# A two-layer graph and expert network on one core: zeros and edge windows written beside the expert sets, gathers and products in another order

## The chip, the core and the metric

The kernel runs on one core of a Trainium2 chip. Its engines are TensorE (PE, matrix products, with its weight loads shown as PEld), VectorE (DVE), ScalarE (ACT), GpSimd (POOL) and SyncE (SP, which here only issues DMAs). The metric is the device time of one execution in microseconds (us). The kernel before takes 968.34 us, the median of five runs between 967.43 and 974.61.

## The reference

There are 3125 nodes of 256 features (float32) and 50000 directed edges, which come sorted by their target `dst`. Cut to what matters, the reference computes

```python
# 1. first graph layer: of each node's incoming edges only the last counts
agg = zeros_like(x).at[dst].set(layernorm(x)[src])
x = x + concatenate((layernorm(x), agg), 1) @ L0_gnn_W.T + L0_gnn_b
# 2. first expert layer: 8 experts of 1024 hidden units, the two best of each node
g = layernorm(x) @ Wg.T + bg;  top 2, softmax over the two
x = x + sum_e combine[:, e] * (relu(layernorm(x) @ W1[e].T + b1[e]) @ W2[e].T + b2[e])
# 3. second graph layer, over all edges
t1  = x @ hW1;  msg = (t1[src] + x[src] * x[dst] @ hW2) / (sqrt(out_deg[src]) * sqrt(out_deg[dst]))
e   = where(in_cnt > 0, t1 + segment_sum(msg, dst), 0) + hb
x   = x + normalized(leaky_relu(e))
# 4. second expert layer: router over 8 experts of 256 hidden units, exact gelu, the two best
x   = x + sum_e combine2[:, e] * (gelu(layernorm(x) @ w1[e] + b1[e]) @ w2[e] + b2[e])
```

## The kernel before

The nodes lie in 25 tiles of 128 rows. Half 0 is tiles 0 to 10, half 1 is tiles 11 to 24. The instructions of each engine run in the order in which the program emits them; this order is written out by hand. All the DMAs named here are issued by SP's queue or, where they gather or scatter by index, by POOL's, and each of these two queues issues in order too.

**The front, 0 to about 60 us.** The edges are read in 13 groups. For each, DVE makes one-hots, PE counts them, and `edge_rows` writes a piece of `etab` (L437), a table in DRAM from which the last edge of a node can be gathered. In the same loop `turn_next` turns the normalized rows of x, multiplies them with the half of the weights that belongs to the neighbour, and writes the products `Z` to the table `ztab` in DRAM (L359). Six DMAs at the start of this block load `wrows` (L389 to 391), the edges laid out as 1560 overlapping windows of 128; L488 writes them to `wtab` in DRAM. `clear_steps` (L247, L250) writes zeros to a table in DRAM, eight groups of 128 rows to a DMA; in this loop it clears the two tables `ytab` (2.9 MB for half 0, 3.5 MB for half 1) into which the first expert layer scatters its results. One step of it follows each group of edges.

**The gathers of half 0, 53 to 123 us.** `picked(t0, t1)` gathers for each tile the rows `er` of `etab` that hold the last edges (`last_edges`, L539, POOL), picks the edge out of them on DVE (`pick_edge`, L545) and makes the neighbours' numbers `nbr` (`neighbours`, to L553). `near(t)` gathers the neighbours' rows of `ztab` (`near_z`, L557, POOL), adds them on DVE (`plus_near`, L575) and takes the statistics of the normalization, for some tiles on ACT. `plus_own(t)` adds the node's own product: four matmuls of PE and one addition on DVE (L566, L569). `other()` is the same product for the next tile of half 1, whose result stays in `hT` and `own_pre` and is read out by ACT (L571, L572). `root` and `finish` normalize up to four tiles on ACT and store them to `xtab` in DRAM (`store_rows`, L590, SP; the three stores are those of tiles 0 to 3, 4 to 7 and 8 to 10). Behind `gate_of_norm` and `sc.best` the routing of half 0 (`route_steps`, its last step on DVE is L870) gives every expert its rows.

**The first expert layer, 123 to 586 us.** 16 sets: the eight experts for half 0 with up to 3 tiles of rows, then the eight for half 1 with up to 4. Before the first set `take` gathers rows of `xtab` (L1021, POOL), which needs all three stores and the routing. In a set a first phase multiplies the turned rows with the first weights (L1067), ACT applies relu into `hid` (L1071), `turn` turns the next set's rows (L1040), and a second phase multiplies `hid` with the second weights (L1081), tile by tile; behind each tile DVE adds the bias (`tensor_add` into `y`, L1086), and POOL scatters `y` to `ytab` (L1090). The weights come by SP (`load_weights`, L951 to 959).

Between these matmuls the program calls `slot()`. Each call advances the generator `beside_first` by one `yield`, that is, it emits the next piece of other work. A set of half 0 has 29 slots (17 in and behind the first phase, 12 in the second), a set of half 1 has 33; there are 496 in all. In this order `beside_first` holds: the rest of half 0's routing; `first_layer_rest`, the first graph layer of half 1; its scores and routing; `windows`, which gathers the windows `win` of `wtab` (L1208) and works on them with DVE (L1217 and the lines behind it, 12 yields after the gathers); `total_in` (its wait for the load `degin` is at L1267, a matmul on PE at L1273); `count_edges`, which builds the matrix of edge counts `atab`; the combination of half 0's results and its statistics (reads `ytab` at L1131, an addition at L1144, the square root at L1542 on ACT); and the addition of the first results of half 1. That last part holds 14 additions on DVE, one for a tile. What is left of the generator after the last slot is emitted then.

**After that.** From 587.86 us PE multiplies the edge counts, loaded by SP (`at`, L1646) and converted by ACT (`wide`, L1796), with the rows (L1800). The fourth of these loads (`at[3]`) reuses memory that the last of the 14 additions reads, and so waits for it. Behind it in SP's queue stand loads of half 1's second results (`second`, L1131). From about 830 us the second expert layer follows.

The clears in the kernel before, one step behind each group of edges:

```python
            if g > 1 and clears and next(clears[0], 0) == 0:
                clears.pop(0)
```

Of the kernel before, what the change touches and what calls it, by code (L numbers as in the profile page):

```python
# [8 lines left out]
F32 = mybir.dt.float32  # L9
# [70 lines left out]
def groups(n, size, first=0):  # L80
    return [(a, min(a + size, n)) for a in range(first, n, size)]
# [28 lines left out]
def gnn_ffn_kernel(ctx: ExitStack, tc: tile.TileContext, x, src_a, src_d, dst_d, dst_row,  # L110
# [121 lines left out]

    wtab = dram.tile([NB, 2, P], I32, name="wtab")

    deg = keep.tile([P, T], F32)
    rooted = keep.tile([P, T], F32)
    none = keep.tile([P, T], I32)
# [141 lines left out]
        nc.vector.tensor_add(X[:, t, :], X[:, t, :], gbt)  # L379

    with tc.tile_pool(name="edges", bufs=2, reuse_waits="tile") as ep:
        WR = NB // 120
        assert WR * 120 == NB
        wrows = ep.tile([120, WR, 2, P], I32, bufs=1)
        for i, a in enumerate((src_a, dst_row)):
            def edges(first, dims):
                return bass.AP(tensor=a.tensor, offset=a.offset + first, ap=dims + [[1, P]])

            nc.sync.dma_start(out=wrows[:119, :, i, :], in_=edges(0, [[WR * B, 119], [B, WR]]))  # L389
            nc.sync.dma_start(out=wrows[119:, :WR - 1, i, :], in_=edges(119 * WR * B, [[1, 1], [B, WR - 1]]))  # L390
            nc.sync.dma_start(out=wrows[119:, WR - 1, i, :], in_=edges(E - P, [[1, 1]]))
        clears = [c for h in range(2) for c in (clear_steps(tabs1[h][1]),)]
        less_mean = ep.tile([P, 2, P], F32, bufs=1)
        iota_2 = ep.tile([P, P], BF16, bufs=1)
        nc.vector.tensor_copy(iota_2, iota_i[:, :P])
# [71 lines left out]
        for g in range(NG):  # L467
            one_hots(g + 2)
            while len(rooted_z) > 1:
                scale_z(*rooted_z.pop(0))  # L470
            if g == NG - 2:
                nc.vector.tensor_scalar(gbase, iota_i[:, :NG], 256.0, None, OP.mult)
            if g == NG - 1:
                last_key(0, 0, NG - 2)
            hot, tiles = hots.pop(g)
            n = min(GE, CD - g * GE)
            pg = bank([P, 2, T], F32, "sb" if g % 2 else "sa", 1)
            for j in range(n):
                nc.tensor.matmul(pg, hot[:, j, :], tiles[:, j, :, :T], start=(j == 0), stop=(j == n - 1))
            nc.scalar.copy(sums[:, g], pg)  # L480
            if 2 <= g < 2 + len(parts_e):
                edge_rows(*parts_e[g - 2])
            if g == 1:
                gates_of_bias()
            while turned[0] < int((g + 1) * STEP):
                turn_next()
            if g == NG - 2:
                nc.sync.dma_start(out=wtab.rearrange("(p r) i l -> p r i l", p=120), in_=wrows)  # L488
            if g > 1 and clears and next(clears[0], 0) == 0:
                clears.pop(0)  # L490
        last_key(1, NG - 2, NG)
        nc.vector.tensor_tensor(last[:, 0], last[:, 0], last[:, 1], OP.max)
        last = last[:, 0]
# [19 lines left out]
        while rooted_z:  # L513
            scale_z(*rooted_z.pop(0))
        nc.vector.tensor_tensor(pre, Z[:, :, DZ + 2:], gates[:, 1:2, :].to_broadcast([P, T, NE]), OP.add)
        assert not any(next(c, 1) is None for c in clears)
    of_turn.close()

    def norm_stats(get, tiles_, tag, mv=None):
# [24 lines left out]
    def pick_edge(pick, i, er, t):  # L544
        nc.vector.scalar_tensor_tensor(pick[:, i, :], er[:, 0, :], node[:, t:t + 1], er[:, 1, :],  # L545
                                       OP.is_equal, OP.mult)
# [779 lines left out]
    with tc.tile_pool(name="ffn", bufs=2, reuse_waits="tile") as fp:  # L1326
# [7 lines left out]
        gp_route = ExitStack()  # L1334
        rp = gp_route.enter_context(tc.tile_pool(name="route", bufs=1, reuse_waits="tile"))
        with tc.tile_pool(name="gnn", bufs=2, reuse_waits="tile") as gp:
            def picked(t0, t1):
                pick = gp.tile([P, 4, P], F32, name="pick", bufs=1)
                for t in range(t0, t1):
                    er[t] = last_edges(eb, t, 8)  # L1340
                    pick_edge(pick, t - t0, er[t], t)
                neighbours(gp, pick, t0, t1)

            loaded1 = {k: [] for k in range(2)}
            sum2 = gp.tile([P, n], F32, bufs=1)

            def near(*tiles_):
                for t in tiles_:
                    plus_near(t, near_z(gp, t, 8))
                    if t in STATS_BY_ACT:  # L1350
                        stat_by_act(gp, mv2, sum2, t)
                    else:
                        stat(X[:, t, :], mv2, t)

            def other():
                t = others.pop(0)
                plus_own(t, own_pre[:, t - n, :])

            def finish(t0, t1):

                scales(mv2, t0, t1)
                xn = gp.tile([P, 4, D], F32, name="xn5")
                for t in range(t0, t1):
                    normed_by_act(xn[:, t - t0, :], X[:, t, :], mv2, t)
                store_rows(tabs1[0][0], 0, t0, t1, xn)

            sc = Scores(rp, 0, 1, pre[:, :n])
            picked(0, 4)
            for t in range(3):
                plus_own(t)  # L1370
            picked(4, 8)
            for t in range(3, 7):
                plus_own(t)
            picked(8, n)
            for t in range(7, n):
                plus_own(t)
            for _ in range(3):
                other()
            near(0, 1, 2, 3)
            root(mv2, 0, 4)  # L1380
            other()
            other()
            near(4, 5)
            finish(0, 4)
            other()
            near(6, 7)
            root(mv2, 4, 8)
            other()
            other()
            near(8, 9)  # L1390
            finish(4, 8)
            near(10)
            root(mv2, 8, n)
            for t in range(n, n + 8):
                er[t] = last_edges(eb, t, 8)
            finish(8, n)
            gate_of_norm(gp, 0, n)
            run(sc.best(0, n))
            for k in range(2):
                for part in range(2):  # L1400
                    load_weights(fp, weights1, HC, slice(k, k + 1), loaded1[k], part)
            routed1[0] = Routed()
            route_rest = route_steps(routed1[0], rp, 0, None, 1, sc)
            for i, _ in enumerate(route_rest):
                if routed1[0].done or i in OWN_AT:
                    while others:
                        other()
                        if not routed1[0].done:
                            break
                if routed1[0].done:  # L1410
                    break
            assert not others
# [51 lines left out]
        def beside_first():  # L1464
            yield from route_rest
            gp_route.close()
            yield from first_layer_rest()
            of_edges.close()
            with tc.tile_pool(name="route", bufs=1, reuse_waits="tile") as rp:
# [3 lines left out]
            with tc.tile_pool(name="codes", bufs=1, reuse_waits="tile") as qp:  # L1473
                qs = qp.tile([P, GW * P, 2], BF16)
                cs = qp.tile([P, GW * P, 2], BF16)
                yield from windows(qs, cs)
                with tc.tile_pool(name="onehots", bufs=2, reuse_waits="tile") as hp:
                    yield from total_in(hp, into)
# [670 lines left out]
```

## Time and profile before

| | value |
|---|---|
| median of five runs | 968.34 us (967.43 to 974.61) |
| the profiled execution: its own time | 971.0 us |
| its span (what the profile shows) | 969.3 us |
| TensorE clock granted, mean over the span | 0.954 of full speed |
| PE busy | 864.3 us, 89% of the span |
| DVE, ACT, POOL busy | 584.4, 401.4, 313.2 us |
| moved by DMA | 162.02 MB, 167 GB/s over the span |
| first matmul of the first expert set | 123.42 us |
| starts of sets 4, 5, 6 | 211.50, 240.58, 272.51 us |
| last bias addition of the first expert layer | 586.23 us |

The profile records one execution. A span is counted from its start, so a time like "at 240.58 us" is a place in this execution. The page cuts the span into 40 slices of 24.2 us and gives for each the busy share in tenths. A wait is shown as the instruction that waited, its line, the engine or DMA and tile that released it, and the sum, number and longest of such waits. A stretch is shown as busy microseconds of each engine with the number of its instructions in brackets, then the granted clock of PE, the busy share of the DMA engines (a little over 1 where records overlap) and GB/s.

### The profile page before, as it was taken

What the parts mean: (1) busy time and instruction counts of PE and PEld (TensorE: products, weight loads), DVE (VectorE), ACT (ScalarE), POOL (GpSimd) and SP (SyncE); (2) the same over time, 40 slices, a digit from 0 to 9 for tenths busy, and PEclk for the clock granted to TensorE, in tenths of its full rate; (3) what the DMA queues carried; (4) which work ended last, traced back from release to release, by engine and by line L of the source; (5) the groups of instructions that cost most, each with busy time, mean ns of one, the idle gap of its engine ahead of it and who ended that gap; (6) DMA issues with size and microseconds to landing.
All of it is one profiled execution on the core that took longest, in us unless ns stands there. A gap on an engine that the chain in (4) does not pass through costs nothing. (4 is left out here: it accounts for less than half of the span.)

```text
span 969.3 us, 13802 instructions
## 1 busy us (share of the span) xinstructions
PE 864.3 (89%) x4803; PEld 641.4 (66%) x4803; DVE 584.4 (60%) x1516; ACT 401.4 (41%) x935; POOL 313.2 (32%) x325
## 2 busy tenths in 40 slices
PE   8937499999699999999999998999999998899980
PEld 7825267666477676676666666789987785657660
DVE  8967566884456555555535526665559665584563
ACT  4833322321136556656632335745564652222110
POOL 2045356622323231341131110011004744274450
PEclk9989699999989999999999999999999999799995
DMA  7993935752456867566354335221013327467964
GB/s 217 275 297 103 294 124 181 236 183 78 137 126 211 304 213 239 197 199 210 125 189 143 107 104 169 69 68 40 20 45 106 120 88 235 118 202 207 312 237 160
DMA packets 124111, 162.02 MB, mean 167 GB/s; under 512 B 21106, under 2 KB 101900, under 8 KB 123911
## 3 DMA queue, kind: packets, MB, share of 16 engines
q1 hardware_dynamic: 104319, 115.05, 37.8%
q0 software_dynamic: 13968, 34.16, 10.8%
q10 hardware_dynamic: 5744, 11.82, 3.2%
q8 instruction: 40, 0.66, 0.3%
q14 instruction: 40, 0.33, 0.1%
HBM read 98.07 MB, written 64.18 MB: 167 GB/s over the span
## 5 line engine op out<-in xcount | busy, mean ns | idle before, releaser
L1081 PE MATMUL y<-w,hid 128*128 128x256 f32 (+4 forms) x1120 | 280.7, 394 | 11.4 <-DVE y L1086 11.1
L1067 PE MATMUL big<-xs,w 128*128 128x380 f32 (+3 forms) x640 | 261.1, 536 | 5.5 <-ACT hid L1071 3.5
L1081 PEld LDWEIGHTS y<-w,hid 128*128 128x128 f32 (+4 forms) x1120 | 199.2, 188 | 44.4 <-DVE y L1086 15.2
L1090 POOL DMA_INDIRECT ytab<-y,put x112 | 125.1, 1117 | 233.2 <-DVE y L1086 212.9
L1071 ACT ACTIVATE hid<-big,bt 128x380 f32<-128x380 f32 (+3 forms) x160 | 97.7, 613 | 222.5 <-PE big L1067 199.2
L1067 PEld LDWEIGHTS big<-xs,w 128*128 128x128 f32 x640 | 114.5, 193 | 68.6 <-issue 28.5
L1796 ACT CAST wide<-at 128x384 fp32r<-128x384 uint8 (+1 forms) x225 | 94.9, 484 | 46.4 <-PE sb L1800 19.1
L1086 DVE TENSOR_TENSOR y<-y,b2t 128x256 f32<-128x256 f32 (+2 forms) x112 | 47.4, 424 | 99.2 <-PE y L1081 98.4
L1021 POOL DMA_INDIRECT g<-xtab,take x56 | 57.9, 1033 | 138.5 <-PE tr L1040 111.2
L1308 PEld LDWEIGHTS <-hq 128*128 128x128 bf16 x800 | 57.1, 98 | 59.6 <-issue 42.6
L1288 DVE TENSOR_TENSOR hq<-qs,iota_b 128x2048 bf16<-128x2048 bf16 x50 | 61.2, 1223 | 55.4 <-PE sb L1308 55.4
L1800 PE MATMUL sa<-wide,parts 128*128 128x512 f32 (+2 forms) x200 | 72.0, 364 | 1.7 <-ACT wide L1796 1.7
L1800 PE MATMUL sb<-wide,parts 128*128 128x512 f32 (+2 forms) x200 | 72.0, 364 | 0.0
L1800 PE MATMUL big<-wide,parts 128*128 128x512 f32 (+1 forms) x300 | 69.5, 381 | 1.7 <-ACT wide L1796 1.7
L1309 ACT CAST at<-sa 128x400 uint8<-128x400 f32 x100 | 49.0, 490 | 40.7 <-PE sa L1308 40.7
L1309 ACT CAST at<-sb 128x400 uint8<-128x400 f32 x100 | 49.0, 490 | 34.6 <-PE sb L1308 33.8
L1041 DVE COPY xs<-tr 128x380 f32<-128x380 f32 (+3 forms) x64 | 35.5, 595 | 45.2 <-PE tr L1040 45.2
L1800 PEld LDWEIGHTS big<-wide,parts 128*128 128x128 f32 x300 | 54.1, 188 | 9.3 <-ACT wide L1796 2.1
L1612 POOL TENSOR_TENSOR XX<-XX,kept 128x256 f32<-128x256 f32 x14 | 10.5, 774 | 122.3 <-DVE kept L533 122.3
L1291 DVE TENSOR_TENSOR hc<-cs,iota_b 128x1600 bf16<-128x1600 bf16 x50 | 49.3, 985 | 0.0
L566 PE MATMUL big<-gWo,hT 128*128 128x264 f32 x100 | 29.1, 450 | 18.8 <-DVE XX L569 14.9
L539 POOL DMA_INDIRECT er<-etab,chunk x25 | 24.6, 984 | 55.3 <-DMA ztab<-Z 37.0
(363 smaller groups left out, 1175.8 us busy)
## 6 DMA issues: line engine op xcount, KB each, us to landing
w<-in_fW SPq DMA_DIRECT2D x32, 1024.0 KB
ytab<-zero_b SPq DMA_DIRECT2D x10, 1024.0 KB
atab<-at ACTq DMA_DIRECT2D x25, 400.0 KB
at<-atab SPq DMA_DIRECT2D x25, 400.0 KB
w<-in_mw SPq DMA_DIRECT2D x32, 256.0 KB
xtab<-zero_b SPq DMA_DIRECT2D x7, 1024.0 KB
y<-ytab SPq DMA_DIRECT2D x12, 512.0 KB
rows<-xtab SPq DMA_DIRECT2D x8, 512.0 KB
```

The source lines that it names most:

```text
L1021: nc.gpsimd.indirect_dma_start(out=g, out_offset=None, in_=tabs[h][0], in_offset=bass.IndirectOffsetOnAxis(ap=routed[h].column(c)[0], axis=0))
L1067: nc.tensor.matmul(ph[:, :many], w1[:, i, c * P:(c + 1) * P], turned[k][:, i, :many], start=(i == 0), stop=(i == KD - 1))
L1071: nc.scalar.activation(hid[:, c, :many], ph[:, :many], act, bias=bt[:, 0, c:c + 1])
L1081: nc.tensor.matmul(py[:m], hid[:, c, j * P:j * P + m], w2[:, c, :], start=(c == 0), stop=(c == nh - 1))
L1086: nc.vector.tensor_add(y[:m], py[:m], b2t[:m])
L1090: dma = nc.gpsimd.indirect_dma_start(out=tabs[h][1], out_offset=into, in_=y[:m], in_offset=None, bounds_check=2 * tokens(layer, h) - 1, oo ...
L1288: nc.vector.tensor_tensor(in_pairs(hq), pairs(qs[:, mine], P), in_pairs(iota_b[:, None, :].to_broadcast([P, n, P])), OP.is_equal)
L1291: nc.vector.tensor_tensor(in_pairs(hc), pairs(cs[:, mine], C), in_pairs(iota_b[:, None, :C].to_broadcast([P, n, C])), OP.is_equal)
L1308: nc.tensor.matmul(pa[:, j], hq[:, g + j, :], hc[:, g + j, :], start=True, stop=True)
L1309: nc.scalar.copy(at[:, :, W * (g0 + g):W * (g0 + g + 4)].rearrange("p i (g w) -> p i g w", w=W), pa.rearrange("p g i w -> p i g w"))
L1796: nc.scalar.copy(wide[:, :j1 - j0, t - t0, :], at[t][:, j0:j1])
L1800: nc.tensor.matmul(sums[g][d][:, :n], parts[:, i, k, d * P:(d + 1) * P], wide[:, i - j0].rearrange("p t l -> p (t l)")[:, :n], start=(i == ...
```

## The change

The work that is computed stays the same; its place in the queues changes.

- The edge windows no longer pass through `wrows`: `window_rows` copies them from DRAM to `wtab` in DRAM with ten DMAs, at the start of the work beside the expert sets, behind the rest of half 0's routing. It yields eight times.
- The zeros of half 0's `ytab` are written behind `finish(4, 8)`, so that in SP's queue they stand between the store of tiles 4 to 7 and that of tiles 8 to 10. The zeros of half 1's `ytab` are written beside the sets, before `windows`, in four yields.
- Gathers of `er` for tiles 0 to 7 come first, then the gathers from `ztab` for tiles 0 to 3, then `er` for 8 to 10, and `ztab` for 4 to 7 and 8 to 10. `pick` has two buffers.
- Own products of half 1 (`other`): 3, 2, 1 and 2 at four places and the rest among the routing before; 2, 3, 2 and 2 now and the rest among the routing. `near(0, 1)` comes before `picked(8, n)`.
- The weights of the first expert are loaded behind `finish(0, 4)`, and only the second expert's behind `sc.best`.

Line numbers of the kernel behind the change are six lower for most of the code (L1217 becomes L1211), and sixteen higher near the end (L1646 becomes L1662).

```diff
@@ -232,6 +232,16 @@
 
     wtab = dram.tile([NB, 2, P], I32, name="wtab")
 
+    def window_rows():
+
+        for i, a in enumerate((src_a, dst_row)):
+            for b0, b1 in groups(NB - 1, 400):
+                nc.sync.dma_start(out=wtab[b0:b1, i, :],
+                                  in_=bass.AP(tensor=a.tensor, offset=a.offset + b0 * B, ap=[[B, b1 - b0], [1, P]]))
+                yield
+            nc.sync.dma_start(out=wtab[NB - 1:, i, :],
+                              in_=bass.AP(tensor=a.tensor, offset=a.offset + E - P, ap=[[P, 1], [1, P]]))
+
     deg = keep.tile([P, T], F32)
     rooted = keep.tile([P, T], F32)
     none = keep.tile([P, T], I32)
@@ -379,17 +389,6 @@
         nc.vector.tensor_add(X[:, t, :], X[:, t, :], gbt)
 
     with tc.tile_pool(name="edges", bufs=2, reuse_waits="tile") as ep:
-        WR = NB // 120
-        assert WR * 120 == NB
-        wrows = ep.tile([120, WR, 2, P], I32, bufs=1)
-        for i, a in enumerate((src_a, dst_row)):
-            def edges(first, dims):
-                return bass.AP(tensor=a.tensor, offset=a.offset + first, ap=dims + [[1, P]])
-
-            nc.sync.dma_start(out=wrows[:119, :, i, :], in_=edges(0, [[WR * B, 119], [B, WR]]))
-            nc.sync.dma_start(out=wrows[119:, :WR - 1, i, :], in_=edges(119 * WR * B, [[1, 1], [B, WR - 1]]))
-            nc.sync.dma_start(out=wrows[119:, WR - 1, i, :], in_=edges(E - P, [[1, 1]]))
-        clears = [c for h in range(2) for c in (clear_steps(tabs1[h][1]),)]
         less_mean = ep.tile([P, 2, P], F32, bufs=1)
         iota_2 = ep.tile([P, P], BF16, bufs=1)
         nc.vector.tensor_copy(iota_2, iota_i[:, :P])
@@ -484,10 +483,6 @@
                 gates_of_bias()
             while turned[0] < int((g + 1) * STEP):
                 turn_next()
-            if g == NG - 2:
-                nc.sync.dma_start(out=wtab.rearrange("(p r) i l -> p r i l", p=120), in_=wrows)
-            if g > 1 and clears and next(clears[0], 0) == 0:
-                clears.pop(0)
         last_key(1, NG - 2, NG)
         nc.vector.tensor_tensor(last[:, 0], last[:, 0], last[:, 1], OP.max)
         last = last[:, 0]
@@ -513,7 +508,6 @@
         while rooted_z:
             scale_z(*rooted_z.pop(0))
         nc.vector.tensor_tensor(pre, Z[:, :, DZ + 2:], gates[:, 1:2, :].to_broadcast([P, T, NE]), OP.add)
-        assert not any(next(c, 1) is None for c in clears)
     of_turn.close()
 
     def norm_stats(get, tiles_, tag, mv=None):
@@ -1334,19 +1328,28 @@
         gp_route = ExitStack()
         rp = gp_route.enter_context(tc.tile_pool(name="route", bufs=1, reuse_waits="tile"))
         with tc.tile_pool(name="gnn", bufs=2, reuse_waits="tile") as gp:
-            def picked(t0, t1):
-                pick = gp.tile([P, 4, P], F32, name="pick", bufs=1)
+            def gather_rows(t0, t1):
                 for t in range(t0, t1):
                     er[t] = last_edges(eb, t, 8)
+
+            def picked(t0, t1):
+                pick = gp.tile([P, 4, P], F32, name="pick", bufs=2)
+                for t in range(t0, t1):
                     pick_edge(pick, t - t0, er[t], t)
                 neighbours(gp, pick, t0, t1)
 
+            z = {}
+
+            def gather_near(t0, t1):
+                for t in range(t0, t1):
+                    z[t] = near_z(gp, t, 8)
+
             loaded1 = {k: [] for k in range(2)}
             sum2 = gp.tile([P, n], F32, bufs=1)
 
             def near(*tiles_):
                 for t in tiles_:
-                    plus_near(t, near_z(gp, t, 8))
+                    plus_near(t, z[t])
                     if t in STATS_BY_ACT:
                         stat_by_act(gp, mv2, sum2, t)
                     else:
@@ -1365,30 +1368,41 @@
                 store_rows(tabs1[0][0], 0, t0, t1, xn)
 
             sc = Scores(rp, 0, 1, pre[:, :n])
+            gather_rows(0, 8)
             picked(0, 4)
-            for t in range(3):
+            gather_near(0, 4)
+            for t in range(4):
                 plus_own(t)
+            for _ in range(2):
+                other()
             picked(4, 8)
-            for t in range(3, 7):
+            gather_rows(8, n)
+            gather_near(4, 8)
+            for t in range(4, 8):
                 plus_own(t)
+            near(0, 1)
             picked(8, n)
-            for t in range(7, n):
+            gather_near(8, n)
+            for t in range(8, n):
                 plus_own(t)
             for _ in range(3):
                 other()
-            near(0, 1, 2, 3)
+            near(2, 3)
             root(mv2, 0, 4)
-            other()
-            other()
+            for _ in range(2):
+                other()
             near(4, 5)
             finish(0, 4)
-            other()
+            for part in range(2):
+                load_weights(fp, weights1, HC, slice(0, 1), loaded1[0], part)
             near(6, 7)
             root(mv2, 4, 8)
-            other()
-            other()
+            for _ in range(2):
+                other()
             near(8, 9)
             finish(4, 8)
+            for _ in clear_steps(tabs1[0][1]):
+                pass
             near(10)
             root(mv2, 8, n)
             for t in range(n, n + 8):
@@ -1396,9 +1410,8 @@
             finish(8, n)
             gate_of_norm(gp, 0, n)
             run(sc.best(0, n))
-            for k in range(2):
-                for part in range(2):
-                    load_weights(fp, weights1, HC, slice(k, k + 1), loaded1[k], part)
+            for part in range(2):
+                load_weights(fp, weights1, HC, slice(1, 2), loaded1[1], part)
             routed1[0] = Routed()
             route_rest = route_steps(routed1[0], rp, 0, None, 1, sc)
             for i, _ in enumerate(route_rest):
@@ -1464,6 +1477,7 @@
         def beside_first():
             yield from route_rest
             gp_route.close()
+            yield from window_rows()
             yield from first_layer_rest()
             of_edges.close()
             with tc.tile_pool(name="route", bufs=1, reuse_waits="tile") as rp:
@@ -1473,6 +1487,8 @@
             with tc.tile_pool(name="codes", bufs=1, reuse_waits="tile") as qp:
                 qs = qp.tile([P, GW * P, 2], BF16)
                 cs = qp.tile([P, GW * P, 2], BF16)
+                for _ in clear_steps(tabs1[1][1]):
+                    yield
                 yield from windows(qs, cs)
                 with tc.tile_pool(name="onehots", bufs=2, reuse_waits="tile") as hp:
                     yield from total_in(hp, into)
```

## The prediction

> **What bounds the kernel now.** I read the page's slices first, for where TensorE (PE) is not busy, then the chain that ended last (it covers only the closing stores, so it decides nothing here), then the time by stretches of a few us, then the waits in the stretches where PE falls short.
>
> ```profile
> PE   8937499999699999999999998999999998899980
> PEclk9989699999989999999999999999999999799995
> DMA  7993935752456867566354335221013327467964
> ```
>
> A slice is 24.2 us. PE is at 9 nearly everywhere from 123 us to the end: there the kernel is bound by PE, and an edit pays only through stretches in which PE stands still or runs at a lower clock. The weak slices are 48 to 121 us (digits 3 7 4: the gathers, with the DMA engines busy), one 6 with a lower clock at 242 to 267 us, and an 8 at 582 us. The first stretch is seen best here:
>
> ```profile
> core 0: us, PE busy (x) PEld busy (x) DVE busy (x) ACT busy (x) POOL busy (x), PEclk, DMA share, GB/s
> 48.00:52.00 4.00, 4.00 (x39) 3.30 (x38) 3.72 (x14) 3.14 (x12) 0.00 (x0) 1.00 1.05 348
> 64.00:68.00 4.00, 0.00 (x0) 0.00 (x0) 0.35 (x1) 0.00 (x0) 1.19 (x2) 0.50 0.97 246
> 76.00:80.00 4.00, 3.48 (x12) 2.48 (x12) 3.01 (x10) 0.00 (x0) 0.93 (x1) 0.82 0.03 10
> 100.00:104.00 4.00, 0.00 (x0) 0.00 (x0) 2.53 (x11) 2.60 (x6) 2.61 (x3) 0.50 0.69 220
> 116.00:120.00 4.00, 0.00 (x0) 0.00 (x0) 0.76 (x3) 0.00 (x0) 3.09 (x4) 0.80 1.07 358
> ```
>
> At 48 to 72 us the DMA engines are the bound (share 0.96 to 1.05): the zeros of both ytab halves, issued at 31.9 to 52 us, are ahead of the last etab, ztab and wtab stores. At 76 to 80 us they stand empty. From 96 to 120 us they are full again, with the weights. The sets of the first expert layer, one row each:
>
> ```profile
> 146.06:167.30 21.24, 21.24 (x88) 15.76 (x86) 13.77 (x36) 4.62 (x8) 15.23 (x16) 1.00 0.61 200
> 211.50:240.58 29.08, 26.53 (x207) 18.43 (x206) 16.53 (x49) 5.99 (x10) 7.19 (x7) 1.00 0.34 105
> 240.58:272.51 31.93, 24.53 (x92) 17.84 (x89) 16.28 (x23) 4.62 (x8) 13.00 (x14) 0.84 0.42 123
> ```
>
> A half-0 set takes 21.24 us when nothing holds it. Set 5 takes 31.93. Its waits:
>
> ```profile
> DVE w L1217 <- DMA win<-wtab,begin_i: 15.3, 1, 15.3
> POOL ytab L1090 <- DVE y L1086: 15.5, 3, 13.4
> PE y L1081 <- DVE y L1086: 7.4, 1, 7.4
> ```
>
> VectorE (DVE) waits in order at L1217 for the seven gathers `win` (243.0 to 251.5 us, landed 256.59). The bias additions L1086 queue behind that wait and behind the window steps of about 1.09 us that follow it; the first runs at 265.54. PE runs out of buffers, stands 7.40 us, and restarts at half clock (16 matmuls in 6.67 us, against 3.62).
>
> **The change, part by part.** Side work advances by one yield per slot among the expert matmuls. window_rows adds 8 yields and the clears of half 1 add 4, so everything behind them comes 12 slots later (8 slots between the two). It adds 10 DMA issues and removes 7. Four places decide.
>
> *Front, 53 to 123 us.* Without the zeros the er rows need not land at 62.7, 67.0, 70.8, and ztab lands about 71 (69.5 to 73) instead of 78.7: the 6.4 MB of zeros alone are 18.5 us of DMA at 345 GB/s, but the rest of this stretch's work (one-hots on DVE to 53 us, first pick at 61.62 at the earliest) hides most of it. Gathers near 0 to 3 start 7 us earlier. But gathers er 8 to 10 now follow them on GpSimd, at 1.25 us an issue, and the picks of tiles 8 to 10 wait for them: they end near 83, as before (83.3). Behind that the chain on ScalarE (ACT) loses one own product of half two (0.5 us) from between; the gate comes 0.5 us sooner (at most 3). New is what stands in SP's queue ahead of the store of xtab rows of tiles 8 to 10: store 0 to 3 (0.52 MB), expert 0's weights (2.23), store 4 to 7 (0.52), the zeros (2.88), its own 0.39, and some 0.4 of er rows: 6.95 MB from about 97.5 us. At the 345 GB/s of the full stretches (337 to 358) that is 20.1 us, plus 2 to 2.5 to land: 120. The first expert gathers L1021 wait for all three stores; they began at 115.48, when the routing (L870) was done, so they begin at about 120. Behind them the first turn comes 6.2 us later as before (115.48 to 121.67): 125.7 instead of 121.67. Loss 4. Ends: 385 GB/s, as in a later stretch full of zeros (xtab<-zero_b, 364 to 410), gives a loss of 2.3; 246, the slowest full row above, gives 28.3 us and a loss of 12.6; a gain of 1 if the store passes the zeros. I take 345 because its rows are of the same mix, weights and zeros, at the same share.
>
> [...]
>
> *Sets 4 and 5.* The win gathers move from slot 1 of set 5 to slot 13, the wait (L1217) from slot 13 to slot 25, behind the bias additions of the second tile. PE then has its buffers while DVE waits. Set 5 loses 31.93 - 21.24 = 10.7; I give back 1.6 to the next wait in line (L1267 `degin`, 8.6 us long in set 6, whose PE users L1273 come with it) and 0.5 to a late addition: gain 8.6 (5 to 10.5). Set 4 loses 29.08 - 26.53 (its PE busy time), of which the exp table load and a wait at L1199 leave its first phase: gain 1.3 (0 to 2). Together 9.9.
>
> *Set 13.* Its first phase takes 16.9 us (501.14 to 518.0) against 12.46 in its neighbours:
>
> ```profile
> DVE XX L1144 <- DMA y<-ytab: 4.3, 1, 4.3
> ACT stats L1542 <- DVE stats L1541: 2.7, 1, 2.7
> PEld big L1067 <- ACT hid L1071: 3.7, 2, 3.2
> ```
>
> The square root L1542 on ACT waits for statistics whose rows come by DMA, loads a table (1.28 us), and the relus L1071 stand behind it; PE waits for hid, then runs at 0.87 and 0.70 of its clock. Twelve slots later L1542 stands behind the last relu of that phase. Gain 4.3 of 4.4 (2 to 4.6).
>
> *End of the experts.* The 14 combines of first results (0.42 us each on DVE) stood all before the last bias addition (586.23). Now four do, and nine are issued after the last slot. The load at[3] (L1646) waits for the last of them: 584.3 before, about 586.9 + 10 x 0.42 = 591.1 now; it landed 2.9 later, so the dense product that began at 587.86 begins at about 594.8, 6.9 later. It had about 3.3 us of stalls of its own in its first 40 us (35.9 of work in 39.2), which the later start absorbs, and `second` loads (L1131), which sit behind at[3] in SP's queue, feed a DVE chain that goes with them: net loss 4 (2.3 to 7).
>
> The clears of half 1 and the DMA copies of wtab in the sets cost nothing: the DMA share there is 0.34 to 0.71. If that cover failed, the weights of a set (1.1 MB a piece, 3.2 us at 345 GB/s) would be late. Losing wrows' six loads (8.86 to 25.9) moves nothing: DVE is busy 19.8 of 20 us there.
>
> Sum: -4 + 9.9 + 4.3 - 4 = +6.2 saved. The profiled run took 971.0 (span 969.3 and 1.7 around it), so 964.8 by its own time. It stands 2.7 above the median of 968.3; none of that lies in a stall that the change moves, so against the median: 962.
>
> **The rivals.**
> *Slower: the zeros in front of the last xtab store.* The other three terms gain 10.2. A later first turn uses that up when the store lands at 125.7 (268 GB/s) and it is slower by over 0.5% from 130.5 on (226 GB/s). For it: 231 and 220 GB/s were what moved at 96 to 104 us. At 220 it is 31.6 us, landing at 131.4, loss 15.9: 974. Against: the share was 0.69 to 0.76 there, so the engines lacked work; full rows with zeros in them gave 337 to 348.
> *No change: the stall keeps its length.* DVE still waits at L1217 for gathers that take 13.6 us to land, and the next bias additions queue behind it, now between tiles two and three or in set 6's second phase. For: the wait is not shortened, only shifted. Against: 25 to 29 slots leave the last addition only. If half of 8.6 and half of 4.3 stay lost: 968.5.
> *Larger gain: the store is not late.* If the er rows and zeros move at 385 and the gate comes 3 us sooner, the front is even and the end loses 2.3: 956.
> The change does what it says; there is no rival in that.
>
> **How the numbers follow.** A measurement can tell about 0.5% (4.8 us) from no change: 963.5 and 973.2 are the bounds. Forecast (958 to 966, middle 962) 0.47; stall kept 0.25; zeros too slow 0.15; larger gain 0.13. Faster: all of the last and 0.37 of the first: 0.50. Slower: the zeros' 0.15 and 0.04 from the stall with a front at its low end: 0.19. Same: 0.31. The range 954 to 975 leaves out the tails of the outer cases, 0.1 each.
>
> **What would show it.** Right: `near` starts at 70 to 73; the third xtab store lands after the routing is done and L1021 starts at 119 to 121; set 5 takes under 24 us with L1217's wait intact but no PE wait at L1081 over 2 us; set 13's first phase under 13 us; L1646's fourth load issued at 590 to 592, first product at 594 to 596. Wrong: L1021 at 115 (no delay) or over 125 (rival one); PE waiting for DVE y in set 5 or 6 again (rival two); at[3] issued at 585, which would mean the combines were not behind the last addition.

## The result, and the profile after

The changed kernel takes 972.97 us (median of 52 runs) where the kernel before takes 970.94 (94 runs): ratio 1.0025, 95% interval 1.0015 to 1.0035. It is slower by about 2.4 us: clear of the noise, but within the half per cent that the prediction counts as no change. Forecast was 962, faster by 0.65%. The profiled execution after took 975.57 us, span 973.8.

The slices of the changed kernel, 24.3 us each:

```profile
PE   7975389998999999999999996999999998899980
PEclk9997679999899999999999998999999999799995
DMA  6143946566546776666445225121013327367964
```

The 6 at 242 us is gone, and a 9 stands there, but an 8 stands one slice earlier (219 us), and a new 6 at 584 us, where before had an 8; the granted clock has an 8 there now, where it had a 9. In the front PE's 3 7 4 has become 7 5 3: the work has moved forward, and the hole ends later. The DMA row has fallen at 24 to 73 us from 9 9 to 1 4, where the zeros and the window rows were written.

What the slices hold in microseconds, from the start of the first matmul of each set to the next (the last column is an experiment, told below):

| stage | before | after | before with twelve empty yields |
|---|---|---|---|
| first expert matmul at | 123.42 | 128.47 | 123.39 |
| sets 0 to 3 | 88.08 | 90.04 | 89.79 |
| set 4 | 29.09 | 30.99 | 30.95 |
| set 5 | 31.93 | 23.83 | 23.83 |
| sets 6 to 12 | 228.63 | 227.86 | 227.95 |
| set 13 | 31.51 | 29.88 | 30.38 |
| sets 14 and 15, to the end of the last bias addition | 54.00 | 53.99 | 54.00 |
| from there to the first dense product | 1.21 | 7.56 | 7.53 |
| first dense product at | 587.86 | 592.62 | 587.82 |

**The front.** The same stretches as shown of before, with the one behind them:

```profile
100.00:104.00 4.00, 0.00 (x0) 0.00 (x0) 3.41 (x15) 1.58 (x3) 0.00 (x0) 0.50 0.95 344
116.00:120.00 4.00, 0.00 (x0) 0.00 (x0) 0.00 (x0) 0.00 (x0) 0.94 (x1) 0.50 1.00 353
120.00:124.00 4.00, 0.00 (x0) 0.00 (x0) 0.00 (x0) 0.00 (x0) 2.97 (x4) 0.50 1.08 338
```

The DMA engines are full from 96 us on, at 344 GB/s and not at 220, and from 116 to 124 us no engine works but POOL, which issues gathers. The wait ahead of them, from the list of waits:

```profile
POOL g L1015 <- DMA xtab<-xn: 21.0, 1, 21.0
```

The store of tiles 8 to 10 was issued at 109.71 us, behind the zeros, and landed when POOL went on, at 118.87; the routing had been done since 113.3.

**Sets 4 and 5.** The same rows as before:

```profile
218.51:249.50 30.99, 25.98 (x146) 18.46 (x144) 17.09 (x58) 6.20 (x10) 7.36 (x8) 0.89 0.65 216
249.50:273.33 23.83, 23.83 (x156) 17.29 (x153) 7.89 (x18) 4.62 (x8) 11.13 (x12) 1.00 0.47 150
```

Set 5 now has PE busy in all of its 23.83 us. Set 4 has PE idle for 5.0 us and its clock at 0.89. POOL's timeline in set 4 and the waits there show whom it waits for:

```profile
235.94 1.03 POOL L1084 DMA_INDIRECT ytab<-y,put  x1 [3.16 <-DVE y L1080]
237.28 0.97 POOL L1015 DMA_INDIRECT g<-xtab,take  x1 [0.31 <-issue]
239.40 1.01 POOL L1084 DMA_INDIRECT ytab<-y,put  x1 [1.14 <-DVE ff L1176]
240.71 0.97 POOL L1015 DMA_INDIRECT g<-xtab,take  x1 [0.30 <-issue]
241.70 0.90 POOL L1178 IOTA w<- 128x896 int32 x1
```

```profile
PE sa L1193 <- DVE less L1187: 4.2, 1, 4.2
DVE first L1180 <- POOL w L1178: 3.4, 1, 3.4
```

`windows` begins with an iota on POOL (L1184 before). There it ran at 218.05 us, in the first phase of the set, with no scatter or gather ahead of it. Twelve slots later it stands behind two scatters and two gathers of the second phase, and POOL, in order, reaches it at 241.70. DVE waits for it, then makes `less`; PE, in order, waits for `less` with expert matmuls behind it, and runs its next matmuls at half clock (four in 2.05 us against 1.11).

**The end.** The waits at 577 to 600 us and the additions on DVE:

```profile
ACT wide L1812 <- DVE XX L1138: 10.0, 1, 10.0
PE sa L1816 <- ACT wide L1812: 8.0, 1, 8.0
```

```profile
584.64 0.42 DVE L1080 TENSOR_TENSOR y<-y,b2t 80x256 f32<-80x256 f32 x1 [1.45 <-PE y L1075]
584.98 4.03 DVE L1138 SCALAR_TENSOR_TENSOR XX<-first,weight,XX 128x256 f32<-128x256 f32 x10
```

Ten additions of first results run behind the last bias addition, then the load they held, and PE stands for 8.0 us.

### The profile page after: what moved, and what is told of

Same layout as the page of the kernel before. It is cut to its first block, busy times and chain, and to the rows that moved or that the text cites. A ratio compares the mean times of both kernels' runs of the same rounds, so it can differ in the third digit from the quotient of the medians.

```text
span 973.8 us, 13826 instructions
## 1 busy us (share of the span) xinstructions
PE 866.6 (89%) x4803; PEld 644.0 (66%) x4803; DVE 584.8 (60%) x1516; ACT 401.7 (41%) x935; POOL 315.8 (32%) x325
## 5 line engine op out<-in xcount | busy, mean ns | idle before, releaser
L1075 PE MATMUL y<-w,hid 128*128 128x256 f32 (+4 forms) x1120 | 275.9, 390 | 5.1 <-DVE y L1080 4.6
L1061 PEld LDWEIGHTS big<-xs,w 128*128 128x128 f32 x640 | 112.9, 192 | 61.3 <-issue 24.3
L1816 PE MATMUL sa<-wide,parts 128*128 128x512 f32 (+2 forms) x200 | 74.2, 374 | 8.0 <-ACT wide L1812 8.0
L1816 PE MATMUL sb<-wide,parts 128*128 128x512 f32 (+2 forms) x200 | 74.2, 374 | 0.0
L1816 PEld LDWEIGHTS sa<-wide,parts 128*128 128x128 f32 x200 | 39.2, 196 | 12.4 <-issue 8.4
```

Source lines behind the costliest of these rows:

```text
L1061: nc.tensor.matmul(ph[:, :many], w1[:, i, c * P:(c + 1) * P], turned[k][:, i, :many], start=(i == 0), stop=(i == KD - 1))
L1075: nc.tensor.matmul(py[:m], hid[:, c, j * P:j * P + m], w2[:, c, :], start=(c == 0), stop=(c == nh - 1))
L1816: nc.tensor.matmul(sums[g][d][:, :n], parts[:, i, k, d * P:(d + 1) * P], wide[:, i - j0].rearrange("p t l -> p (t l)")[:, :n], start=(i == ...
```

## The experiments

Two theories. "Order": the change is a sum of a few stalls which moved when the side work moved by twelve slots and the store by three transfers; each can be taken away by itself, at its price in the table. The rival: transfers moved in among the sets slow them, or what is mended in one place is lost in the next; then single edits give little. A ratio is to the kernel before on the same chip.

**Before with twelve empty yields.**

```diff
             gp_route.close()
+            for _ in range(8):
+                yield
             yield from first_layer_rest()
...
+                for _ in range(4):
+                    yield
                 yield from windows(qs, cs)
```

> The kernel before with twelve empty yields, eight behind the rest of half 0's routing and four before windows: the slots of the side work shift as in the change, and nothing else is moved. Theory 'order' (the change is a sum of a few stalls that were moved): the first expert matmul stays at about 123.4 us, set 4 gets the wait behind GpSimd's iota and takes about 31 us, set 5 takes about 24 instead of 31.9, set 13 about 29.9 instead of 31.5, the dense product begins about 7.5 us behind the last bias addition instead of 1.2. In sum 3 to 4 us faster than before. Rival 'traffic' (zeros and window rows moved in among other transfers slow the sets down, the shift of slots is worth nothing): within 1 us of before.

Measured: 970.23 us, ratio 0.9985 (0.9959 to 1.0011). Its rows for sets 4 and 5:

```profile
213.18:244.13 30.95, 25.96 (x145) 18.46 (x144) 17.07 (x58) 6.20 (x10) 7.38 (x8) 0.89 0.31 102
244.13:267.96 23.83, 23.83 (x156) 17.30 (x153) 7.97 (x18) 4.62 (x8) 11.13 (x12) 1.00 0.45 150
```

Every place is as "order" has it, the sets as in the changed kernel to within 0.5 us, with no new transfers (102 and 216 GB/s in set 4 make no difference to its time). So what happens in the sets is the shift alone, not the traffic. The time by itself would not have told: its interval, from 4.0 us faster to 1.1 slower, holds what either theory expected. The sum was mis-sized: the sets up to the last bias addition take 6.4 us less, and 6.3 are given back before the first product, which begins at the same time as before.

**The change without its yields**, that is, its front alone:

```diff
-            yield from window_rows()
+            for _ in window_rows():
+                pass
...
                 for _ in clear_steps(tabs1[1][1]):
-                    yield
+                    pass
```

> The changed kernel without its twelve new yields (window rows and zeros of half 1 issued in one go at their places): the front as in the change, the slots as before. Theory 'order': first expert matmul at about 128, set 4 about 29, set 5 near 32, set 13 31.5, product 1.2 us behind the last bias addition: 4 to 5 us slower than before, 2 to 3 us slower than the change by the sum of its places. Rival: equal to the change within 1 us (since the shift of slots alone came out at nothing, 0.9985).

> The changed kernel without its twelve new yields, so that the slots are as before and the front as in the change. Theory 'order': first expert matmul at about 128, set 4 about 29, set 5 about 31.5, set 13 31.5, product 1.2 us behind the last bias addition: 4 to 5 us slower than before by the front alone, ratio 1.004 to 1.005, or less by what the stalls behind the product absorb (1.4 us).

The first of these two, and three more kernels told at the end of this section, ran on another chip, where the kernel before takes 1022.24 us; the ratio there was 0.9998 (0.9977 to 1.0019). The second measured 974.13 us, ratio 1.0040 (1.0022 to 1.0058): the front costs 3.9 us, with 2.1 to 5.6 as the interval. Its first expert gather and its first product:

```profile
117.59 0.94 POOL L1015 DMA_INDIRECT g<-xtab,take  x1 [20.21 <-DMA xtab<-xn]
```

```profile
589.79 0.47 PE L1817 MATMUL sa<-wide,parts 128*128 128x512 f32 x1 [1.79 <-ACT wide L1813]
```

First matmul at 126.86 us, set 4 at 29.09, set 5 at 30.79, no long wait ahead of the product. Set 13 took 30.00 us and not 31.5: PE stands as long as before (2.57 us), but the 16 matmuls behind that take 6.55 us instead of 8.19. With set 5, too, 1.1 us shorter, the first product is only 1.9 us later than before in this execution. Front (+0.40%) and shift (-0.15%) add up to the change's +0.25%; each of the two is known to no better than 0.2 to 0.3%, so that this good a fit is partly luck.

**Zeros behind the store of tiles 8 to 10.**

```diff
-            for _ in clear_steps(tabs1[0][1]):
-                pass
             near(10)
...
             finish(8, n)
+            for _ in clear_steps(tabs1[0][1]):
+                pass
```

> The changed kernel with the zeros of half 0 issued behind the store of tiles 8 to 10 instead of ahead of it. Theory 'order': the first expert gather begins at about 115.5 us (the end of the routing) instead of 118.9, the first expert matmul 3 to 4 us earlier, the time 3 to 4 us below that of the change. Rival (the gathers, not the store, set the start): the first expert matmul within 1 us of 128.5.

Measured: 967.48 us, ratio 0.9967 (0.9942 to 0.9992). The first gather, and how long the gathers took to land:

```profile
113.36 0.94 POOL L1015 DMA_INDIRECT g<-xtab,take  x1 [14.85 <-DVE no L864]
```

```profile
DMA to landing us min/median/max: 5.5/6.0/6.6
```

The gather waits for the routing again. The first matmul comes at 123.33, 5.1 us earlier, and the time is 5.6 us below that of the change by the two ratios (3 to 4 expected). But the gather began 2.1 us earlier than in the kernel before (115.48), and the first matmul is where it was (123.42). The first set needs three gathers, and PE turns their rows as they land. Before, then here:

```profile
121.67 1.69 PE L1040 MATMUL tr<-ident,g 128*128 128x128 f32 x6 [6.35 <-DMA g<-xtab,take]
```

```profile
119.99 1.00 PE L1034 MATMUL tr<-ident,g 128*128 128x128 f32 x2 [7.76 <-DMA g<-xtab,take]
122.10 1.10 PE L1034 MATMUL tr<-ident,g 124*128 124x124 f32 x4 [1.12 <-DMA g<-xtab,take]
```

The first turn is 1.7 us earlier, but the third tile's rows, gathered at 115.85, land only at 122.06. Before they were gathered at 117.98, and their first turn is at 122.25: 6.2 us against 4.3 at most. Of the kernel before, the trace has landings only of gathers issued from 120.48 on, when the DMA rate had fallen to 57 to 246 GB/s (2.7 to 3.4 us for those up to 124.23). Its first gather, beside weights at 358 GB/s, took up to 6.2. The kernel with twelve empty yields shows the dependence within one trace: gathers issued at 114.12 to 116.62 us, beside 334 to 344 GB/s, took 5.6 to 5.9 us, and the one issued at 121.63, at a DMA share of 0.43, took 2.8. So in these traces a gather took longer while such transfers were under way.

**The iota early.** It is emitted behind `first_layer_rest`, into a tile of its own; no slot moves.

```diff
             of_edges.close()
+            ip = of_iota.enter_context(tc.tile_pool(name="counts", bufs=1, reuse_waits="tile"))
+            firsti = ip.tile([P, GW, P], I32, name="firsti")
+            nc.gpsimd.iota(firsti, pattern=[[W, GW * P]], base=0, channel_multiplier=0)
```

> The changed kernel with the one iota of the window starts (GpSimd) emitted before half 1's scores instead of in windows; same slots. Theory 'order': the 4.2 us for which PE stands in set 4, and the half clock behind it, shrink to under 1 us, set 4 takes about 26 us instead of 31, the time is 4 to 5.5 us below that of the change. Rival (DVE is late there anyway): set 4 within 1 us of 31.

Measured: 967.05 us, ratio 0.9980 (0.9956 to 1.0003), against the change's 1.0025. Set 4 and the iota:

```profile
218.18:243.48 25.30, 23.84 (x145) 17.06 (x144) 17.21 (x58) 6.20 (x10) 6.80 (x7) 1.00 0.65 215
```

```profile
214.07 0.90 POOL L1485 IOTA firsti<- 128x896 int32 x1
```

Set 4 is 5.7 us shorter, at full clock, and set 5 is no longer than it was (23.82). The time is 4.4 us below that of the change by the two ratios. One instruction of 0.90 us on an engine that is busy a third of the time cost that. Sets 4 and 5 together take 49.1 us; before 61.0, in the change 54.8.

**First results twelve slots earlier.** The eight yields at the loads of `at` are taken out, and four of the twelve ahead of the additions.

> The changed kernel with twelve yields taken out behind the combination of half 0 (eight at the loads of at, four ahead of the additions of first results), so that the 14 additions stand in the slots they had before. Theory 'order': at[3] loads as early as before, the dense product begins 1 to 2 us behind the last bias addition instead of 7.5, the half clock behind that is gone; 4.5 to 6 us below the change's time. Rival (the statistics of half 1 bind the product, a later start is absorbed): under 2 us.

Measured: 968.30 us, ratio 0.9976 (0.9957 to 0.9994), so 4.8 us below the change by the two ratios. The first product:

```profile
586.11 0.47 PE L1814 MATMUL sa<-wide,parts 128*128 128x512 f32 x1 [1.64 <-ACT wide L1810]
```

It begins 1.2 us behind the last bias addition.

**Three places together** (zeros behind the store, iota early, first results early):

> The changed kernel with three places mended together: the zeros of half 0 behind the last xtab store, the iota of the window starts early, the additions of first results twelve slots earlier. Theory 'order': the places add up. First expert matmul at about 123.4 us (4.5 to 5 less than the change), set 4 at 25.3 (5.7 less), product 1.2 us behind the last bias addition (6.4 less): 12 to 16 us below the change, ratio to before about 0.988. Rival (what is mended in one place is lost in the next): ratio to before 0.995 or more.

Measured: 958.75 us, ratio 0.9883 (0.9857 to 0.9909): 11.4 us faster than before, 13.8 faster than the change. One by one the three places gave 5.6, 4.4 and 4.8 us, 14.8 in all: the places add up, and this version beats both. First matmul at 122.08 us, set 4 at 25.31, product 1.2 us behind the last addition. Behind the front its slices have no 6 left:

```profile
PE   8976399999999999999999998999999998899880
```

**The kernel before with the yields and the same two mends** differs from the last one in the front, and in where the zeros and the window rows are written.

> The kernel before with the twelve empty yields and the two mends behind the front (iota early, additions of first results twelve slots earlier); front and zeros as before. It differs from the one with three places mended only in the front: gathers' order, own products, zeros and window rows. If the change's front is worth nothing once the store is not held (first expert matmul 123.3 in both), the two are equal within 1.5 us, ratio to before about 0.988. If the earlier gathers are worth something, this one is 2 us or more slower.

Measured: 961.67 us, ratio 0.9905 (0.9880 to 0.9930). Beside the kernel with three places mended, on the same chip and with six runs of each, that is 2.9 us more by the medians (0.8 to 5.6 as a 95% interval of the means), as "worth something" has it. In the traces the first matmul comes at 124.09 us here and at 122.08 there. But these traces are of the slowest execution here and the fastest there, and sets 6 and 7, far behind the front, also differ, by 2.7 us, with a clock of 0.98 and 0.96 here. So the change's front is worth something once the store is free; how much, the runs don't settle.

**Loads early.** As the kernel with three places mended, but the first expert's weights and the zeros of half 0 are issued behind `gather_near(0, 4)`.

> As the kernel with three places mended, but the first expert's weights and the zeros of half 0 stand in SP's queue behind the ztab stores, before every xtab store, so that they move at 64 to 85 us, where the DMA engines had a share of 0.03 at 76 to 80. If the transfers that are still under way at 113 us hold the first expert's gathers (5 to 6 us to land), they land in under 3.5 us here and the first expert matmul comes at 119 to 121 us: 2 to 4 us below the kernel with three places mended. If the gathers of near rows (69.8 to 87 us, 2.8 us to land) are held up as much, the gain is gone: within 1 us of it.

Measured: 962.61 us, ratio 0.9929 (0.9904 to 0.9954): slower than the kernel with three places mended, by 0.46%. The gathers of er rows up to 80 us:

```profile
DMA to landing us min/median/max: 2.9/5.4/5.8
```

With three places mended their median was 3.1. The picks wait for them, the xtab stores begin at 99.88 instead of 94.18 us and the routing ends at 118.0 instead of 112.6. What the early load frees is not on the path; what it delays is. And the first three gathers of the expert sets, issued from 118.20 us on, were still turned only 5.1 us after their issue, with window rows alone beside them (DMA share 0.40 and 0.41 at 116 to 124 us), so that the first matmul came at 127.06 instead of 119 to 121.

**Three kernels on the slower chip.**

> The changed kernel with four places mended together: the zeros of half 0 behind the last xtab store, the window rows copied just ahead of the zeros of half 1 (their eight yields stay in place), the iota of the window starts early, and the additions of first results twelve slots earlier. Theory 'order': the places add up; first expert matmul at 121 to 123.4 us instead of 128.5, set 4 about 25.3 us, product 1.2 us behind the last bias addition: 13 to 16 us below the change, 10 to 13 below before, some 958 us. Rival (what is mended in one place is lost in the next): under 8 us below the change.

> The changed kernel with the zeros of half 0 behind the last xtab store and the window rows copied in set 4. With the zeros alone moved, the first expert gather began at 113.36 us but took 5.5 to 6.6 us to land (2.7 to 3.4 before), so that the first expert matmul stayed at 123.33. If the window rows are what slows these gathers, they land in under 3.5 us again and the first expert matmul comes at about 121. If the zeros and weights ahead in SP's queue do it, they take 5 to 6 us still and it stays at about 123.

> The changed kernel with the zeros of both halves back among the edges, where they were before, and four empty yields in their place in the sets; the gathers' order, the own products and the window rows stay as changed. Theory 'order': ztab lands late again (first near gather at about 78 us instead of 69.8), the store of tiles 8 to 10 is not held, the first expert gather begins at 113 to 116 us, and the sets are as in the change: 3 to 5 us below the change. If the window rows slow the first gathers, they land in 5 us here too, with no zeros about; if zeros do it, in 3 us.

Measured: ratios 1.0028 (1.0008 to 1.0048), 1.0053 (1.0030 to 1.0077) and 1.0069 (1.0049 to 1.0088). These times are inconclusive: the changed kernel was not measured on this chip, the first matmul comes late there in all four kernels (132.48 to 135.76 us), and all three lose 14 to 15 us in set 1, which took 21.23 in every kernel on the other chips. Behind the front the places are as expected (four mended: set 4 25.31, product 1.5 us behind the last addition). PE in the kernel with four places mended:

```profile
170.05 1.54 PE L1061 MATMUL big<-xs,w 128*128 128x380 f32 x4 [1.13 <-ACT hid L1065]
174.29 2.56 PE L1061 MATMUL big<-xs,w 128*128 128x380 f32 x4 [2.69 <-issue]
178.48 2.90 PE L1061 MATMUL big<-xs,w 128*128 128x380 f32 x4 [1.63 <-ACT hid L1065]
```

Four matmuls every 4.2 us, with waits that in part the profile puts to no instruction ("issue"). The kernel without yields has no such stretch in set 1 there. What it is was not found.

Two things in these traces can be read all the same. The first is what slows the first gathers. With the zeros back among the edges only window rows move beside them (DMA share 0.57 and 0.44 at 124 to 132 us), and the rows of the first gather are turned 5.1 us after its issue:

```profile
123.61 0.94 POOL L1018 DMA_INDIRECT g<-xtab,take  x1 [25.87 <-DVE no L867]
```

```profile
128.75 0.47 PE L1037 MATMUL tr<-ident,g 128*128 128x128 f32 x1 [6.27 <-DMA g<-xtab,take]
```

With zeros and weights beside them and the window rows late, it is 5.7 (issued at 123.88, turned at 129.54). So either is enough, and taking away one of them alone frees little. The second is a forecast that failed: with the zeros back the first near gather was to begin at about 78 us and began at 70.14, as without them on this chip (69.91). So the zeros alone were not what held the near gathers. Whether late window rows alone are worth anything in time, no run shows.

## Why the prediction was wrong

The four steps of the sum, then the rest, by the profiled executions; the sum forecast 6.2 us saved, the first 600 us show 3.4 lost. Of these 9.6 us, 3.7 are in sets 4 and 5, 2.0 in sets 0 to 3, 1.9 in sets 6 to 13, and 1.0 each in the front and at the end. No single step turned the sign: with the miss in sets 4 and 5 alone, the largest, 2.5 us would still have been saved.

*Front, -4: right in its number, in part by luck.* The store landed at 118.87 (119 to 121), at 344 to 386 GB/s from 100 us on (345 taken), the first turn came at 124.85 (125.7). The first matmul is 5.05 us later, 1 more than forecast, because the third tile is turned 2.4 us behind the first (0.6 before): its rows, gathered at 121.37 with 338 GB/s under way, were turned 5.9 us on, where before it was 4.3. The front alone measured 3.9, on the wide interval given above. The sum counts all 6.95 MB ahead of the landing of the store. That was the author's estimate, as were the 2 to 2.5 us to land: no run shows in which order the DMA engines take a queue's transfers, nor that term by itself. What the runs show is the store issued at 109.71 behind the zeros and landed 9.16 later, and a first gather at 113.36, when the routing was done, with the store ahead of the zeros. The rival with slower zeros did not come. Near gathers began at 69.77 (70 to 73), but not for the reason given: with the zeros back in their old place they began at 70.14, though on the other chip. What still differs there from the kernel before is the order of the gathers and own products, and the window rows, which no longer pass through `wrows` to `wtab` ahead of the last `ztab` stores; which of these it is, no run shows.

*Sets 4 and 5, +9.9: this step failed.* Set 5 gained 8.10 (forecast 8.6). Set 4 was to gain 1.3, since the exp table load and a wait at L1199 were to leave its first phase. It lost 1.9. The wait did leave the first phase, but the sum took it to cost nothing where it went, and did not follow the iota ahead of it into POOL's queue, where twelve slots put it behind the second phase's scatters and gathers. The iota early shows its size: 5.7 us. The rival "the stall keeps its length" had the kind right (a wait that moves), but the wrong wait: that at L1211 shrank to 1.6 us and held nobody.

A second part of it: the prediction counted half clock where a stall goes (set 5, set 13), but not behind a stall that comes. In the changed kernel PE ran slowly behind 4.2 and 8.0 us of idling (granted clock 0.58 at 244.01 to 249.50 us, 0.50 at 592.62 to 596.60), and at full clock behind 1.65 (set 2, 1.00 at 184.23 to 185.61). Set 13 lies between, and has no fixed price: before, behind 2.4 us, 16 matmuls took 8.19 us where the 16 ahead of the wait took 6.39; with the front alone, behind 2.57 us, they took 6.55.

*Set 13, +4.3: the stall went, but new ones came in set 6.* The relus no longer wait for the square root:

```profile
DVE XX L1138 <- DMA y<-ytab: 13.1, 1, 13.1
ACT hid L1065 <- PE big L1061: 4.5, 8, 0.9
```

DVE waits longer for its rows, and no relu stands behind it; no wait of PE is listed. The set is only 1.63 shorter, and its first phase takes 14.9 us instead of under 13, since nine groups of the edge counts moved into it from set 6. A group costs PE 0.20 to 0.24 us (sets with 33, 30 and none take 35.03, 34.44 and 27.11 us), so without them it would be 3.4 to 3.8 shorter. Three more groups went from set 7 to set 12. In sets 6 and 7 PE's busy time fell by 2.4 us, their time by only 1.4: set 6 now has 1.2 us of PE idle (0.2 before), behind ACT's copies of the turned windows and for `all_in`.

*End, -4: right in place, 1 us short.* Forecast was the product at 594.8, 8.2 us behind the end of the last addition (586.65); it came 7.56 behind it, which costs 6.35 against before. Then the first ten product matmuls ran at half clock, 0.43 us apart instead of 0.23: at 599 us the trace stands 6.7 us behind that of before. The later start absorbs 3.3 of that, as forecast: from 617 to 790 us it stands 3.3 to 3.4 behind. What the sum left out is the half clock, 1.9 us.

*Sets 0 to 3, nothing: 2 lost.* PE waits 1.65 us for a relu in set 2 (0.68 before), by the shift. The other 1.1 is the first phase of set 0, which took 12.41 us before and 12.6 to 14.0 in every other profile on these chips, 13.24 with the slots of before. PE comes out of the front at half clock there (0.50), and three to eight matmuls run before it rises; so this is more likely scatter than the change.

The median of 968.34 from which the forecast subtracted came from five runs; 94 gave 970.94, and the profiled execution at 971.0 was not above it. That is 2.6 us of a miss of 11. The profiled execution after lost another 3.2 us between 797 and 816 us, with a granted clock of 0.82 over that stretch (1.00 before), for which no cause was found, and part of it came back; its 975.57 lies 2.6 above its median.

## What to carry to other kernels

When side work is shifted along a written order, follow every instruction of the first step behind the shift on every engine's queue, the cheapest ones too: 0.90 us on GpSimd held TensorE for 4.2 us and half its clock behind that. A shift removes a stall at one place and pays elsewhere, so list all the waits that a shift by so many slots moves, and let the work that depends on the end of the sequence keep its place from the end. Put stores that someone waits for ahead of zeros in their queue: here that was worth 5.6 us by the two ratios.

## What the runs showed of the hardware

A gather of 128 rows landed in 2.7 to 3.0 us where little else moved (the near rows of the changed kernel, at a DMA share of 0.33 to 0.38 from 72 to 88 us) and took 5.1 to 6.6 beside zeros, weights or the copies of window rows, the last even at a share of 0.40. An earlier issue by 2.1 us thus gained nothing at the first matmul. Behind 4.2, 7.4 and 8.0 us of idling TensorE ran at a granted clock of 0.58, 0.54 and 0.50 over the next 4 to 6.5 us (set 4 and the end after, set 5 before), behind 1.65 and 1.66 at 1.00 (set 2 after, the end before), and behind 2.44 and 2.57 in set 13 once slowly and once not. On the slower chip four matmuls took 2.90 us behind 1.63 and 1.54 behind 1.13. And one chip ran the kernel before 5% slower than the others (1022.24 against 970.67 us), with stalls of its own, so that a ratio from there does not carry over.
